# Batch 0 opened in a hand-written order of all engines, with a fence behind it

## The chip, the core and the metric

The kernel runs on one core of a Trainium2 chip. The core has five engines, each with its own instruction stream, executed in order: TensorE (PE in the profile, its weight loads PEld), VectorE (DVE), ScalarE (ACT), GpSimd (POOL) and SyncE (SP), which here issues transfers. Engines wait for each other through semaphores. The metric is the device time of one execution in microseconds (us); lower is better.

## The reference

Two layers over x of 4 batches x 512 tokens x 256 channels, all in float32. Cut to what matters:

```python
# layer 0: both branches start from xn = layernorm(x)
phi_q, phi_k = elu(q) + 1, elu(k) + 1              # q, k, v: 256 -> 256 each, with bias
context = phi_q * cumsum(phi_k * v, axis=1) * 0.25
attn = context @ Wo.T + bo
logits = (rms(xn) * norm_w) @ Wc.T / clip(temperature, 0.1)   # 512 "genes" per token
w = softmax(top_k(logits, 32))
e = sum_k w_k * genes[idx_k]                       # 32 numbers per token
ffn = tanh(e @ Wd.T) * xn' * (e @ Wu.T) * scale    # xn' = rms(xn) * norm_w
x = x + attn + ffn
# layer 1: both branches start from xn = layernorm(x)
q, k, v = split(rms(xn) @ w_qkv.T)
y = sigmoid(rms(q)) * cumsum(exp(rms(k)) * v) / (cumsum(exp(rms(k))) + 1e-6)
u, g = split(y @ w_swiglu.T)                       # 2 x 1024
mix = xn + (u * silu(g)) @ w_out.T
moe = two of 16 experts per token (176 wide) + a shared expert (352 wide)
x = x + mix + moe
```

The cumulative sums run along the 512 tokens of a batch, so the second half of a batch needs a carry from the first.

## The kernel before

Tokens lie in tiles of 128 (`P`), four (`NT`) to a batch; x stays in SBUF as `xs` for the whole kernel. The work is written as Python generators, and `together` takes steps from several of them in turn, so that their instructions stand interleaved in the program; a scheduler then orders each engine's instructions, and may move an instruction ahead of others that it does not depend on. So statistics of later batches can stand between steps of batch 0.

The generators:
- `layer0(b, i0, nt)` (L231) does layer 0 for `nt` tiles of batch b from tile i0: statistics and normalisation (`statistics` L201, `normalise` L218, on DVE), turned rows `xnT` through PE and ACT (`turn` L224), then for each tile `logits` (L293: four matmuls of which two reach one bank of PSUM at a time), `top` (L303: four rounds of max and match_replace on DVE, then the weights `e`), a share of the attention branch (`phi` L260, `attend_kv` L272, `attend_q` L285) and `express` (L320: `e` turned, multiplied with genes, then with Wd and Wu, tanh, and four GpSimd operations that add bias and branch to `xs`); at last `out` (L343), the out-projection added to `xs`.
- `mix(b, i0, nt)` (L368) is the mixing of layer 1: statistics, turned rows `xn1T`, q, k, v, sums, `yT`, and the router's weights. At its end it enters `(xnT, yT)` in `made` (L464).
- `dense(busy)` (L574) is the shared expert and the gated projection of layer 1, by halves of a batch (256 tokens). A half has 11 steps (`NC`): three chunks of the shared expert, which need only `xn1T` (weights `sgu`), and eight of the gated projection, which need `yT` (weights `wugt`). A step is `up` (four matmuls `gu`, L584, 256 columns each) and, two steps behind, `down` (two matmuls `acc`, L604). There are 8 halves, 88 steps in all; `d(n)` takes n of them.
- `route` and `scatter` (L467, L549) sort the tokens by expert; `scatter` writes 32 sets of rows to DRAM from GpSimd's queue. `experts` (L783) reads them in pairs of tiles (`xg`), turns them (L712), and multiplies with an expert's weights, `pu` (L749) and `py` (L770).
- The tail runs what is left of `dense`; in it GpSimd gathers the experts' rows 32 times (L885), asked for by step number, and DVE adds them to `xs` (L896), also by step number.

The calls that set the order are few:

```python
    together(a(0, 0, 2))
    together(m(0, 0, 2), a(0, 2, 2))
    ...
    together(m(0, 2, 2), a(1, 0, 4), d(NC))
    together(m(1, 0, 4), a(2, 0, 4), d(NC))
    together(m(2, 0, 4), a(3, 0, 4), d(NC))
    ...
    together((scatter(), 33), d(14))
    run_all(islice(dd, 2 * NC - 19))
    ...
    together((experts(), NP2 + 2))
```

Batch 0 comes in halves, so that the first mixing can start after two tiles. PSUM is in four banks `pm` (`bank`, L195), three `gu` and one `acc`. All loads are issued on SP's queue in the order of L103 to L151; small ones (`nwc`, `tmp1`, `bqkv`, `scl`) stand between large ones. DVE scales `wct` with the norm's weights (L157). The halvings of `wot1` and `sdn` (L648 to L650, on ACT) stand behind batch 0.

Of the kernel before, what the change touches and what calls it, by code (L numbers as in the profile page):

```python
# [2 lines left out]

# [51 lines left out]
def tile_two_layers(  # L55
# [53 lines left out]
    G.memset(ones, 1.0)  # L109

    load_x(0)
# [4 lines left out]
    nc.sync.dma_start(nwc, norm_w.rearrange("(h p) -> p h", p=P))  # L116
    tmp1 = wp.tile([P, 1], F32, name="tmp1")
    nc.sync.dma_start(tmp1, temperature.partition_broadcast(P))
    nc.sync.dma_start(wqkv, wqkv0.rearrange("(h p) e -> p h e", p=P))
    bqkv = wp.tile([P, 6], F32, name="bqkv")  # L120
    nc.sync.dma_start(bqkv, bqkv0)
# [7 lines left out]
    nc.sync.dma_start(scl, scale.partition_broadcast(P))  # L129
# [23 lines left out]
    V.tensor_scalar(nbqk, bqkv[:, 0:4], -1.0, None, ALU.mult)  # L153
    bqkv1 = wp.tile([P, 4], F32, name="bqkv1")
    V.tensor_scalar(bqkv1, bqkv[:, 0:4], 1.0, None, ALU.add)
    for h in range(NH):
        V.tensor_scalar(wct[:, h], wct[:, h], nwc[:, h : h + 1], None, ALU.mult)  # L157
    rtemp = wp.tile([P, 1], F32, name="rtemp")
    V.tensor_scalar(rtemp, tmp1, 0.1, None, ALU.max)
    V.reciprocal(rtemp, rtemp)  # L160
# [40 lines left out]
    def statistics(pool, b, i0, nt):  # L201

        mv = pool.tile([P, NT, 2], F32, name="mv")
        rs = pool.tile([P, 2, NT], F32, name="rs")
        ve = pool.tile([P, NT], F32, name="ve")
        for i in range(nt):
            bs = pool.tile([P, 6], F32, name="bs")
            V.bn_stats(bs, xs[:, b, i0 + i])
            V.bn_aggr(mv[:, i], bs)
        V.tensor_scalar(rs[:, 0, 0:nt], mv[:, 0:nt, 1], LN_EPS, None, ALU.add)  # L210
# [3 lines left out]
        S.activation(rs[:, :, 0:nt], rs[:, :, 0:nt], AF.Sqrt)  # L214
        V.reciprocal(rs[:, :, 0:nt], rs[:, :, 0:nt])
# [15 lines left out]
    def layer0(b, i0, nt):  # L231

        W = nt * P
        mv, rs = statistics(io, b, i0, nt)
        xn = io.tile([P, NT, D], F32, name="xn")
        normalise(xn, b, i0, nt, mv, rs)

        sl = io.tile([P, 2, NT], F32, name="sl")
        V.tensor_scalar(sl[:, 0, 0:nt], rs[:, 1, 0:nt], rtemp, None, ALU.mult)
        V.tensor_scalar(sl[:, 1, 0:nt], rs[:, 1, 0:nt], scl, None, ALU.mult)  # L240
        yield
        xnT = io.tile([P, NH, L], F32, name="xnT")
        for h in range(NH):
            S.copy(xnT[:, h, 0:W], turn(xn, nt, h * P))  # L244
        yield


        def project(c):
            pm = bank()[:, 0:W]
            for h in range(NH):  # L250
                T.matmul(  # L251
                    pm,
                    wqkv[:, h, c * P : (c + 1) * P],
                    xnT[:, h, 0:W],
                    start=(h == 0),
                    stop=(h == NH - 1),
                )
            return pm

        def phi(c):  # L260

            pm = project(c)
            e = io.tile([P, L], F32, name="phi", bufs=3)[:, 0:W]
            S.activation(e, pm, AF.Relu, bias=nbqk[:, c : c + 1], scale=-1.0)
            S.activation(e, e, AF.Exp, scale=-1.0)
            V.scalar_tensor_tensor(e, pm, bqkv1[:, c : c + 1], e, ALU.add, ALU.max)
            return e

        ctxT = one.tile([P, NH, L], F32, name="ctxT")
        cums = {}  # L270

        def attend_kv(h):  # L272
            fk = phi(2 + h)
            pv = project(4 + h)
# [9 lines left out]

        def attend_q(h):  # L285
            fq = phi(h)
            V.scalar_tensor_tensor(ctxT[:, h, 0:W], fq, QSCALE, cums[h], ALU.mult, ALU.mult)


        rden = io.tile([P, NT], F32, name="rden")  # L290
        exT = one.tile([P, L], F32, name="exT")

        def logits(i):  # L293
            pl = bank()
            for h in range(NH):
                T.matmul(  # L296
                    pl, xnT[:, h, i * P : (i + 1) * P], wct[:, h], start=(h == 0), stop=(h == NH - 1)
# [5 lines left out]
        def top(i, lg):  # L303
            tp = io.tile([P, NACT], F32, name="top")
            rep = io.tile([P, NG], F32, name="rep")
            for r in range(NACT // 8):
# [3 lines left out]
                if r == 0:  # L310
                    nm = io.tile([P, 1], F32, name="nm")
                    V.tensor_scalar(nm, tp[:, 0:1], sl[:, 0, i : i + 1], -1.0, ALU.mult, ALU.mult)
                    e = io.tile([P, NG], F32, name="e")
                    S.activation(e, lg, AF.Exp, bias=nm, scale=sl[:, 0, i : i + 1])
            den = io.tile([P, 1], F32, name="den")
            V.scalar_tensor_tensor(e, rep, TAKEN, e, ALU.is_equal, ALU.mult, accum_out=den)
            V.reciprocal(rden[:, i : i + 1], den)
            return e

        def express(i, e):  # L320
# [4 lines left out]
            S.copy(wT.rearrange("p c t -> p (c t)"), pw)  # L325
            px = bank()
            for c in range(NGC):
                T.matmul(px[c * GD : (c + 1) * GD, 0:P], gn[:, c], wT[:, c], start=True, stop=True)
            S.copy(exT[:, i * P : (i + 1) * P], px[:, 0:P])
            du = bank()  # L330
            T.matmul(du, exT[:, i * P : (i + 1) * P], wdut, start=True, stop=True)
            dn = io.tile([P, D], F32, name="dn")
            S.activation(dn, du[:, 0:D], AF.Tanh, scale=rden[:, i : i + 1])
            cf = io.tile([P, 1], F32, name="cf")
            V.tensor_tensor(cf, rden[:, i : i + 1], sl[:, 1, i : i + 1], ALU.mult)
            V.scalar_tensor_tensor(dn, du[:, D : 2 * D], cf, dn, ALU.mult, ALU.mult)
            xw = io.tile([P, D], F32, name="xw")
            G.tensor_tensor(xw, xn[:, i], nwb, ALU.mult)
            G.tensor_tensor(dn, dn, xw, ALU.mult)
            G.tensor_tensor(xs[:, b, i0 + i], xs[:, b, i0 + i], bob, ALU.add)  # L340
            G.tensor_tensor(xs[:, b, i0 + i], xs[:, b, i0 + i], dn, ALU.add)

        def out(i):  # L343
            ao = bank()[:, 0:D]
            for h in range(NH):
                T.matmul(  # L346
                    ao, ctxT[:, h, i * P : (i + 1) * P], wot[:, h], start=(h == 0), stop=(h == NH - 1)
                )
            V.tensor_tensor(xs[:, b, i0 + i], ao, xs[:, b, i0 + i], ALU.add)


        parts = [lambda h=h, f=f: f(h) for h in range(NH) for f in (attend_kv, attend_q)]
# [610 lines left out]
```

## Time and profile before

| what | value |
|---|---|
| median of 3 runs | 581.01 us (578.38 to 581.03) |
| the profiled execution | 576.85 us, its span 575.1 us |
| instructions in the profile | 7191 |
| weight loads on PE | 383.5 us (67%) |
| moved by transfers | 46.76 MB, mean 81 GB/s |

The page's first part gives each engine's busy time; its second cuts the span into 40 equal slices, each digit being the busy share of a slice in tenths, with the clock that PE was granted below. In the timeline a line has a start and a duration in us, then engine, line of the kernel and operation, the tile written and the tiles read, the shape and the count; in brackets stands how long the engine was idle before it and what ended the wait. A matmul in float32 leaves two records, a turn of 128x128 one. A line can belong to a helper: L228 is the turn wherever `turn` is called.

### The profile page before, as it was taken

To read this page: it belongs to the slowest core of one execution; us is meant where nothing else is said; L and a number is where in the kernel's file an instruction comes from. 1 tells how busy PE (TensorE), PEld (TensorE's weight loads), DVE (VectorE), ACT (ScalarE), POOL (GpSimd) and SP (SyncE) were. 2 spreads that over 40 slices of the span, in tenths; PEclk is the share of its full clock that TensorE was granted. 3 is DMA by queue.
4 is the path that set the end of the run, shared out by engine and by line. 5 is a ranking of instruction groups with operands and counts; after the bars stand their busy time and mean duration, and the time that the engine had idled before them with its cause. 6 is when DMAs were issued, how large, how long until landed. Compare 5 with 4: busy or idle time off the path is not lost.

```text
span 575.1 us, 7191 instructions
## 1 busy us (share of the span) xinstructions
PE 527.4 (92%) x2324; PEld 383.5 (67%) x2324; DVE 370.3 (64%) x985; ACT 228.4 (40%) x517; POOL 173.6 (30%) x214
## 2 busy tenths in 40 slices
PE   3557989989999999999999989997999999999996
PEld 1344656558656676566677768886677777788885
DVE  4979999998796797967981499232222222236653
ACT  1452746562655825458344611111433333321110
POOL 1235132354222423223352322774000000016660
PEclk9788899999999999999999999999899999999999
DMA  5995000000000000000045630233333332114441
GB/s 165 376 375 206 1 1 0 2 0 1 0 2 0 0 1 2 0 1 1 1 144 158 202 100 11 103 109 126 94 110 101 102 109 92 55 66 129 123 143 40
DMA packets 37736, 46.76 MB, mean 81 GB/s; under 512 B 3936, under 2 KB 34240, under 8 KB 37440
## 3 DMA queue, kind: packets, MB, share of 16 engines
q1 hardware_dynamic: 34624, 37.87, 20.2%
q0 software_dynamic: 3072, 8.39, 4.8%
q8 instruction: 20, 0.33, 0.2%
q14 instruction: 20, 0.16, 0.1%
HBM read 27.64 MB, written 18.61 MB: 80 GB/s over the span
## 4 chain that ended last, share of the span: by engine, by line
PE 54%; DVE 22%; POOL 8%; ACT 7%; issue 4%; DMA 4%; SPq 0%; POOLq 0%; ACTq 0%; DVEq 0%
PE gu L584 12%; PE pu L749 9%; PE acc L604 7%; PE py L770 6%; PE pm L391 5%; DVE rep L309 4%; DVE top L308 4%; POOL xrows L552 3%; PE pt L712 3%; POOL ys L885 3%; PE pm L251 3%; PE pm L296 2%; PE pm L228 2%; PE pm L346 2%; DVE sums L437 2%
## 5 line engine op out<-in xcount | busy, mean ns | idle before, releaser
L584 PE MATMUL gu<-yT,wugt 128*128 128x256 f32 x512 | 126.0, 381 | 0.0
L584 PEld LDWEIGHTS gu<-yT,wugt 128*128 128x128 f32 x512 | 94.9, 190 | 18.9 <-issue 7.2
L588 ACT ACTIVATE th<-gu 128x256 f32<-128x256 f32 (+1 forms) x88 | 33.5, 382 | 122.7 <-PE gu L584 116.1
L885 POOL DMA_INDIRECT ys<-yrows,slot x32 | 30.7, 961 | 133.4 <-PE gu L584 117.9
L604 PE MATMUL acc<-wot,hid 128*128 128x256 f32 x256 | 66.2, 381 | 0.4
L595 POOL TENSOR_TENSOR hid<-hid,th 128x256 f32<-128x256 f32 (+1 forms) x44 | 34.1, 779 | 101.2 <-ACT hid L594 97.9
L590 DVE SCALAR_TENSOR_TENSOR th<-th,gu 128x256 f32<-128x256 f32 (+1 forms) x88 | 36.1, 412 | 41.6 <-ACT th L588 41.5
L749 PE MATMUL pu<-wex,xgT 128*128 x168 | 58.3, 470 | 0.8 <-DMA xg<-xrows 0.8
L604 PEld LDWEIGHTS acc<-wot,hid 128*128 128x128 f32 x256 | 48.1, 190 | 9.3 <-POOL hid L595 2.0
L251 PE MATMUL pm<-xnT,wqkv 128*128 128x512 f32 (+1 forms) x120 | 46.7, 530 | 3.9 <-ACT qk L398 1.7
L584 PE MATMUL gu<-xn1T,sgu 128*128 128x256 f32 (+1 forms) x192 | 47.3, 382 | 1.4 <-ACT hid L594 1.3
L758 DVE TENSOR_TENSOR hb<-pu,hb 128x176 f32<-128x176 f32 x42 | 14.3, 341 | 51.9 <-ACT hb L757 51.9
L391 PE MATMUL pm<-w,xn1T 128*128 128x512 f32 (+1 forms) x128 | 45.9, 502 | 0.1
L584 PEld LDWEIGHTS gu<-xn1T,sgu 128*128 128x128 f32 (+1 forms) x192 | 33.8, 181 | 9.5 <-ACT hid L594 2.6
L770 PE MATMUL py<-wex,hgT 128*128 x168 | 39.8, 379 | 0.0
L391 PEld LDWEIGHTS pm<-w,xn1T 128*128 128x128 f32 x128 | 24.7, 194 | 21.7 <-issue 17.5
L251 PEld LDWEIGHTS pm<-xnT,wqkv 128*128 128x128 f32 x120 | 23.8, 201 | 21.9 <-issue 13.2
L770 PEld LDWEIGHTS py<-wex,hgT 128*128 128x128 f32 x168 | 31.8, 190 | 7.9 <-issue 0.4
L552 POOL DMA_INDIRECT xrows<-xn,slot x32 | 30.9, 966 | 19.7 <-DVE th L590 10.3
L749 PEld LDWEIGHTS pu<-wex,xgT 128*128 128x128 f32 x168 | 29.4, 195 | 10.5 <-ACT xgT L726 1.2
L762 DVE COPY hgT<-pt 128x512 f32<-128x512 f32 x21 | 14.5, 691 | 30.0 <-PE pt L712 30.0
L296 PE MATMUL pm<-wct,xnT 128*128 128x512 f32 x64 | 33.4, 659 | 0.3 <-ACT xnT L244 0.2
(163 smaller groups left out, 872.2 us busy)
## 6 DMA issues: line engine op xcount, KB each, us to landing
xrows<-zero SPq DMA_DIRECT2D x1, 6016.0 KB, 23.3
wex<-in_w_gate_up_dram SPq DMA_DIRECT2D x8, 704.0 KB, 4.7
xg<-xrows SPq DMA_DIRECT2D x21, 256.0 KB, 2.7
yrows<-yg SPq DMA_DIRECT2D x21, 256.0 KB, 2.1
xs<-in_x_dram SPq DMA_DIRECT2D x4, 512.0 KB, 8.0
wugt<-in_wug_dram SPq DMA_DIRECT2D x1, 2048.0 KB, 11.9
wex<-in_w_down_dram SPq DMA_DIRECT2D x4, 512.0 KB, 4.8
out_dram<-xs SPq DMA_DIRECT2D x7, 256.0 KB, 2.8
```

What stands on the lines that cost most here:

```text
L251: T.matmul(pm, wqkv[:, h, c * P : (c + 1) * P], xnT[:, h, 0:W], start=(h == 0), stop=(h == NH - 1),)
L296: T.matmul(pl, xnT[:, h, i * P : (i + 1) * P], wct[:, h], start=(h == 0), stop=(h == NH - 1))
L391: T.matmul(o[:, 0:n], xnT[:, h, i * P : (i + 1) * P], w1[:, h, at : at + n], start=(h == 0), stop=(h == NH - 1),)
L552: sc = G.indirect_dma_start(out=xrows, out_offset=bass.IndirectOffsetOnAxis(ap=slot[:, k, i : i + 1], axis=0), in_=xn1[:, i // NT, i % NT] ...
L584: T.matmul(gu[0:m, k], w[:, h, at : at + m], ins[which][:, h], start=(h == 0), stop=(h == NH - 1))
L588: S.activation(th[0:m], gu[0:m, 0], AF.Tanh, scale=0.5)
L590: V.scalar_tensor_tensor(th[0:m], th[0:m], 1.0, gu[0:m, 0], ALU.add, ALU.mult)
L595: G.tensor_tensor(hid[0:m], hid[0:m], th[0:m], ALU.mult)
L604: mm = T.matmul(acc[:, t], hid[0:m, t * P : (t + 1) * P], dw[0:m, dc], start=(n == 0 and t == 0), stop=(n == NC - 1), skip_group_check=True,)
L749: T.matmul(pg[:, 0 : 2 * NI], xT[:, i, h], wex[:, bass.ds(at[i] + h * 2 * NI, 2 * NI)], start=(h == 0), stop=(h == NH - 1),)
L770: mm = T.matmul(py[:, i * D : (i + 1) * D], hT[:, i, h], wex[:, bass.ds(at[i] + EW - (2 - h) * D, D)], start=(h == 0), stop=(h == 1),)
L885: G.indirect_dma_start(out=ys[:, asked], out_offset=None, in_=yrows, in_offset=bass.IndirectOffsetOnAxis(ap=slot[:, k, n : n + 1], axis=0) ...
```

## The change

Batch 0 is no longer given as two `layer0` generators. `parts0` holds the pieces of layer 0 for a range of tiles as separate functions, and `opening` calls them in an order written out by hand, for both halves of batch 0 up to the turned rows of the first mixing (two tiles). Within `tc.manual_schedule` PE, DVE, ACT and GpSimd keep that order; `tc.no_sync_barrier()` is a fence for the scheduler, which moves nothing across it. What is left of the first mixing and of batch 0's second half then runs through `together` as before, with three dense steps; the other batches are `layer0(b)` over four tiles.

Along with it: x of batch 0 is loaded in two pieces, and four small loads go from SP's queue to ACT's; `ones` is set by DVE instead of GpSimd, `wct` is scaled by GpSimd instead of DVE; matmuls of the identity into an unused bank (`keep_up`) stand in four places; the expressed rows of two tiles are made together (`express`); the two parts of `made` are entered as each becomes ready; two more dense steps run between scatter and experts (`2 * NC - 17`), and the adds of gathered rows in the tail are asked for earlier by step number (15 for 17).

```diff
-    G.memset(ones, 1.0)
-
-    load_x(0)
+    V.memset(ones, 1.0)
+
+    nc.sync.dma_start(xs[:, 0, 0:2], x[0, 0:HB].rearrange("(t p) d -> p t d", p=P))
...
     nc.sync.dma_start(wct, wc.rearrange("(h p) g -> p h g", p=P))
...
-    nc.sync.dma_start(nwc, norm_w.rearrange("(h p) -> p h", p=P))
+    nc.scalar.dma_start(nwc, norm_w.rearrange("(h p) -> p h", p=P))
+    nc.sync.dma_start(xs[:, 0, 2:4], x[0, HB:].rearrange("(t p) d -> p t d", p=P))
...
-        V.tensor_scalar(wct[:, h], wct[:, h], nwc[:, h : h + 1], None, ALU.mult)
+        G.tensor_scalar(wct[:, h], wct[:, h], nwc[:, h : h + 1], None, ALU.mult)
...
+        def express(i, wTs):
+            px = bank()
+            for c in range(2):
+                for g in range(NGC):
+                    j = g % 2 * 2 + c
+                    T.matmul(
+                        px[g * GD : (g + 1) * GD, 0:P], gn[:, j], wTs[g // 2][:, j], start=(c == 0), stop=(c == 1)
+                    )
+            exT = io.tile([P, P], F32, name="exT")
+            S.copy(exT, px[:, 0:P])
+            dus = [bank(), bank()]
+            for t, du in enumerate(dus):
+                half = slice(t * P // 2, (t + 1) * P // 2)
+                T.matmul(du, exT[half], wdut[half], start=True, stop=True)
+            for t, du in enumerate(dus):
+                expressed(i + t, du)
...
+    def opening():
+        k = batch0(0)
+        p, q = parts0(0, 0, 2, k), parts0(0, 2, 2, k)
+        idle = ps_a.tile([P, 2, D], F32, name="acc")
+
+        def keep_up(n):
+            for _ in range(n):
+                T.matmul(idle[:, 0, 0:P], ident, ident, start=True, stop=True)
+
+        keep_up(14)
+        mv = moments(io, 0, 0, 2)
+        rs = spread(io, mv, 2)
+        mv2 = moments(io, 0, 2, 2)
+        V.reciprocal(rs[:, :, 0:2], rs[:, :, 0:2])
+        normalise(k.xn[:, 0:2], 0, 0, 2, mv, rs)
+        p.turn_in()
+        rs2 = spread(io, mv2, 2)
...
+        p.scales(rs)
+        V.reciprocal(rs2[:, :, 0:2], rs2[:, :, 0:2])
+        normalise(k.xn[:, 2:4], 0, 2, 2, mv2, rs2)
...
+        q.scales(rs2)
+        lg = {0: p.logits(0), 1: p.logits(1)}
+        held = {}
+        for two in ((2, 4), (0, 3), (5, 1)):
+            pm = ps_d.tile([P, 2, HB], F32, name="gu")
+            for j, c in enumerate(two):
+                held[c] = p.project(c, pm[:, j])
+        low = {2: p.decay(2, held[2])}
+        e0 = p.top(0, lg[0])
+        for c in (0, 3):
+            low[c] = p.decay(c, held[c])
+        q.turn_in()
+        low[1] = p.decay(1, held[1])
+        lg[2] = q.logits(2)
+        w0 = p.turn_genes(e0)
+        e1 = p.top(1, lg[1])
+        lg[3] = q.logits(3)
+        keep_up(8)
+        w1t = p.turn_genes(e1)
+        p.sum_kv(0, p.phi(2, held[2], low[2]), held[4])
+        p.context(0, p.phi(0, held[0], low[0]))
+        kh = p.phi(3, held[3], low[3])
+        p.express(0, [w0, w1t])
+        keep_up(8)
+        p.sum_kv(1, kh, held[5])
+        p.context(1, p.phi(1, held[1], low[1]))
+        for c in range(0, DFF // P, 2):
+            S.mul(wot1[:, c : c + 2], wot1[:, c : c + 2], 0.5)
...
+        p.out(0)
+        p.out(1)
+        keep_up(12)
+        m0 = mix(0, 0, 2)
+        next(m0)
+        next(m0)
+        return m0, q.rest(lg)
...
-    together(a(0, 0, 2))
-    together(m(0, 0, 2), a(0, 2, 2))
...
-    together(m(0, 2, 2), a(1, 0, 4), d(NC))
...
+    kinds = mybir.EngineType
+    with tc.manual_schedule(engines={kinds.PE, kinds.DVE, kinds.Activation, kinds.Pool}):
+        m0, second = opening()
+    tc.no_sync_barrier()
+    run_all(islice(m0, 2))
+    together((m0, 4), (second, 8), d(3))
+    together(m(0, 2, 2), a(1), d(NC - 3))
+    together(m(1, 0, 4), a(2), d(NC))
+    together(m(2, 0, 4), a(3), d(NC))
...
-    run_all(islice(dd, 2 * NC - 19))
+    run_all(islice(dd, 2 * NC - 17))
...
-        while added < 2 * NTT and 17 * added <= 32 * (step - 3):
+        while added < 2 * NTT and 15 * added <= 32 * (step - 3):
```

`p` stands for tiles 0 and 1, `q` for tiles 2 and 3. `moments` and `spread` are the two halves of `statistics`, up to the square root on ACT; `decay` is the part of `phi` on ACT, `phi` what DVE does behind it; `turn_genes` is the turn of `e` with its copy; `rest` is the loop over tiles of `layer0`, with logits that are there already taken over.

## The prediction

> **What bounds the kernel now.** The page first. TensorE (PE) is busy for 92% of the span, and the two rows of slices say where it is not:
>
> ```profile
> PE 527.4 (92%) x2324; PEld 383.5 (67%) x2324; DVE 370.3 (64%) x985; ACT 228.4 (40%) x517; POOL 173.6 (30%) x214
> PE   3557989989999999999999989997999999999996
> DVE  4979999998796797967981499232222222236653
> PEclk9788899999999999999999999999899999999999
> ```
>
> The gaps of PE lie in the first six slices (14.4 us each) and in slice 28; there DVE is full, and the clock dips. Busy is not work, though: PE's records are long when its clock is low. So I made a ledger from the groups by line with their shapes kept apart: records in a stretch times what one takes when PE is warm (from the chain: eight 128x256 in 1.73 us, so 0.215; 0.43 for 512 columns, 0.11 for 128, 0.30 for 352). Time less that work is time lost: 9.7 us by 10 us, 24.0 by 40, 30.6 by 55, **36.2 by 85**; then nothing (33.5 to 36.5) as far as 280; 4.6 in 320 to 360; **7.2 in 398 to 410**; 5.4 in the last 15 us. Of 575.1 us some 520 are work. The change touches the two bold places.
>
> The timeline of PE, then that of DVE (start, duration):
>
> ```profile
> 9.32 1.14 PE L228 MATMUL pm<-ident,xn 128*128 128x128 f32 x4 [9.32 <-DVE xn L220]
> 10.49 5.72 PE L296 MATMUL pm<-wct,xnT 128*128 128x512 f32 x8
> ...
> 23.90 1.09 PE L323 MATMUL pm<-ident,e 128*128 128x128 f32 x4 [5.10 <-DVE carry L282]
> ...
> 44.25 1.22 PE L228 MATMUL pm<-ident,xn 128*128 128x128 f32 x4 [5.81 <-DVE xn L220]
> ```
>
> ```profile
> 14.92 0.69 DVE L308 MAX8 top<-lg 128x8 f32<-128x512 f32 x1 [2.88 <-ACT lg L300]
> ...
> 43.78 3.80 DVE L220 TENSOR_SCALAR xn<-xs,mv,rs 128x256 f32<-128x256 f32 x6
> ...
> 54.16 0.68 DVE L308 MAX8 top<-lg 128x8 f32<-128x512 f32 x1
> ```
>
> DVE is the opening's chain: top-32 of two tiles from 14.9, first mixing normalised at 44.4 (the first two of those six), top-32 of tiles 2 and 3 only at 54.2. From 39.6 to 54 DVE worked largely for batches 1 to 3: twelve bn_stats (0.33 each), eight normalisations and what goes with them, some 14 us with two scalings at 72.8, while PE idled.
>
> The seam to the experts:
>
> ```profile
> 396.26 0.96 POOL L552 DMA_INDIRECT xrows<-xn,slot  x1 [0.30 <-issue]
> ```
>
> ```profile
> 396.82 1.03 PE L604 MATMUL acc<-wot,hid 128*128 128x256 f32 x4
> 401.66 1.09 PE L712 MATMUL pt<-ident,xg 128*128 128x128 f32 x4 [3.81 <-DMA xg<-xrows]
> 403.50 2.71 PE L749 MATMUL pu<-wex,xgT 128*128 x4 [0.75 <-DMA xg<-xrows]
> ```
>
> Scatters run on POOL every 1.26 us, the last at 396.3; PE is out of dense work at 397.9, waits 3.8 us, and goes on at half speed (2.71 for what later takes 1.19).
>
> **The opening by the new order.** In-order engines, durations from those rows.
> - First rows: 256 KB instead of 512 come first. Loads of 256 KB (xg) land in 2.7 us, so 0.8+2.7 = 3.5, against 4.3. Moments and spread of two tiles 1.4, square root 0.3: 5.2. But the second moments stand in DVE's queue ahead of the first reciprocal, and their rows arrive behind wct: the same 1 MB had landed at 5.8 (wct: 1.3+4.5). So 5.8+0.8+0.15, reciprocal by 6.75, two normalisations by 8.0 at 0.62 each (the x6 row, beside POOL; 0.35 alone). Turn and copy 0.8: logits from 8.4 instead of 10.5.
> - wct's scaling goes from DVE (0.48 each) to POOL, whose form the trace does not show. nwc, moved to ACT's queue ahead of the table load, lands about 0.8+4.6 = 5.4. Nearest row: POOL's two-input 128x512 at 1.37, two by 8.2. The Trainium skill ("GPSIMD Engine Reference", Engine selection) speaks against it: elementwise belongs on VectorE, about twice as fast for two inputs; one-input is "roughly line-rate", which gives about 0.5 each. Either is in time for 8.4, so 0; late by more, it is on the chain one for one. Its "SBUF — State Buffer" (Who interferes with whom) is harsher: a 2-port DVE op is shut out for the whole POOL instruction, so the two normalisations could wait until 8.2, +1.2. The row's 0.62 is taken. Four issues of 0.47 and the table load of 1.28 leave ACT free at 4.0, before the root at 4.9. SP loses those four, so what it issues behind comes 0.5 to 2 earlier. The other three small loads, wqkv and ones on DVE land before their first reader: 0.
> - Fourteen dummy matmuls warm PE: two logits matmuls 1.7 (cold 2.9), lg copy 0.6. **Top-32 of tile 0 starts at 11.1, not 14.9.**
> - Written out, the two top-32s do not interleave. A dependent round took 1.52 (maxima at 25.96 and 27.48) against 1.27 when two alternate; with scale and sum 6.9 each: 18.0 and 24.9. The six projections (5.1 of PE), second turns and logits lie beside this.
> - Then the turn of e1 0.55, copy 0.6, px 0.4, exT 0.3, two du 1.8 (warm), tanh, dn: DVE at 28.8 and 29.7; phi, kv, scan, context of the halves end at 32.0, beside it.
> - POOL is late next: xw and the bias, done early before, now stand in order: from 28.9 seven ops of 0.73 end at **34.0** (before: 1.55 behind dn). Out-projection (32.1 to 33.9) is covered.
> - Residual add 0.5, statistics 1.5, square root 0.4, normalisation by 37.4; turned rows 38.4. The six halvings, now in ACT's order between tanh and the root, wait for wot1 (15.3+14.0 = 29.3, as tanh ends) and sdn (30.2), and need 3.2 plus 1.3 of table load: done by 34, needed at 36. The fence shows no instruction or wait of its own in the program's order.
>
> So first-mixing normalisation stands at 37.4 against 44.4, and top-32 of tiles 2 and 3 follows at once: **37.4 against 54.2, 16.8 us earlier**. From there to the end of the first mixing (85.0) DVE does the same, less 1.3 (a scaling of batch 2), plus 1.8 (moments of batch 1): 68.7, so 16.3 gained with the same PE work done. The 42 dummies (9 us warm) lie in waits.
>
> The clock: the skill ("TensorE: Matmul & The Clock Gate", Part 1) holds the warm-up below 1% of a typical span, here 5.8 us, so warming could bring no more; the records show 34.0 busy for 26.1 of work by 60 us, 7.9 of stretch alone. I take the records. If dummies do not warm it, about 5.5 of cold turns, logits, du, out return on the new chain: gain 10.8.
>
> **The debt.** Of the 14 us hoisted, 1.8 is counted. Batch 1 still owes about 4 in a stretch (85 to 120) with DVE 34 of 35 us busy and PE full; batches 2 and 3 about 7 where DVE is 80 to 90% busy. PE has eight dense steps (2.59 each) as cover. Between 0 and 11 I take 3.5, since PE has lost nothing there: **opening 12.8**.
>
> **Seam and tail.** 2NC-17 instead of 2NC-19 moves two steps, 5.2 us, ahead of the experts. Scatters still start with the same step, xg had landed 3.8 after PE stopped, so the wait goes and PE stays warm; the copy to xgT (0.75) and 0.2 stay: **6.2 of 7.2**. The tail has 20 steps. Gathers are asked for at the same steps, so the last still issues with step 18:
>
> ```profile
> 560.44 0.94 POOL L885 DMA_INDIRECT ys<-yrows,slot  x1 [0.40 <-DVE th L590]
> ```
>
> It lands near 563.0, and its add (15*added) stands in DVE's queue ahead of the last hidden product, which PE wants at 562.8: add 0.5, product 0.4, so **-0.7** (0 to -3).
>
> Halves expressed in pairs: eight exT copies (0.27) less on ACT, same PE columns; the first tile waits for the second. 0 behind dense steps, up to 3 at one stage's end without. `made` set early: three sgu steps were ahead before too, 0.
>
> Sum: 12.8 + 6.2 - 0.7 = 18.3. Profiled execution: 576.85 (span 575.1), so 558.5. The median of the runs is 581.01, 0.7% above: **562.5**.
>
> **Rivals.**
> 1. The debt is paid in full: DVE's idle up to 85 us was 14.1, the new order idles about 12 by its fence. For: DVE is as full as PE to 120. Against: slack later. 16.3-11 = 5.3; with 5.5 for the rest 10.8: 570. Chance 0.19.
> 2. Seam gives nothing, because scatters slip with the steps or the tail waits on gathers (1.26 us each leave six us in twenty steps): 12.8 alone, 568. For: the chain there is all POOL. Against: pacing showed only 0.3. Chance 0.10.
> 3. Debt hidden whole: 16.3+5.5, 559. Chance 0.15.
> 4. Slower: without the hoist, each later batch's statistics fall on its own chain (normalise, turn, logits, top-32), ahead of PE's cover. It decides from a payment of 22 us, and the hoisted rows sum to 14, so one and a half times over: at 25, 584. Chance 0.03.
> 5. The change does not do what it says: the order shortens the opening, but PE loses as much behind the fence, and the seam stays: 580. Chance 0.02.
>
> The forecast has 0.51. Its own range is 557 to 567. Landing times, POOL's two ops (+1.2) and cold PE (5.5) widen it; 556 to 571 leaves out the last two rivals and the edges. A measurement tells 0.5% (2.9 us): faster 0.94, same 0.02, slower 0.04.
>
> **What would show it.** First top-32 near 11, POOL's last add near 34, first-mixing rows turned near 38, next top-32 straight behind. L317 at 0.43 each, not 0.72. Lost work by the end of the first mixing near 20, then 3 to 4 more before 140. No wait for xg at the seam, first pu near 1.2. The last gather behind the last but one step, one short wait of PE at the end. Wrong if top-32 starts after 13, or if PE idles behind the fence for over 6 us.

## The result, and the profile after

| | changed kernel | kernel before |
|---|---|---|
| median of 7 runs | 574.62 us (572.46 to 576.04) | 580.86 us (578.38 to 581.52) |
| ratio, 95% interval | 0.9909 (0.9889 to 0.9929) | |
| profiled execution | 574.23 us, span 572.5 | 576.85 us, span 575.1 |

By the ratio of the runs the change brings about 5.3 us (the medians lie 6.2 apart); 18.3 were forecast, as 562.5 us with a range of 556 to 571. One run of the experiment `again` below, 915.54 us at a granted clock of 0.557, was slow and stands in none of the figures. The page of the changed kernel (busy times, then the rows of slices, 14.3 us each):

```profile
PE 531.6 (93%) x2408; PEld 390.4 (68%) x2408; DVE 370.1 (65%) x984; ACT 233.8 (41%) x515; POOL 172.8 (30%) x215
PE   6969789979899999999999989978999999999995
DVE  5979989999897897968942687313322222225554
PEclk8999989999999999999999999997999999999999
```

PE's gaps of the first six slices are smaller, but there is one again at the scatters (the 8, 9, 9, 7, 8 right of the middle of PE's row).

The opening, in the timelines of PE, DVE and POOL (start, duration, engine, line, operation):

```profile
1.64 4.73 PE L439 MATMUL acc<-ident 128*128 128x128 f32 x28 [1.64 <-POOL ident masks.py:199]
9.33 0.87 PE L235 MATMUL pm<-ident,xn 128*128 128x128 f32 x4 [2.95 <-DVE xn L227]
10.49 5.37 PE L317 MATMUL pm<-wct,xnT 128*128 128x512 f32 x8 [0.29 <-issue]
```

```profile
7.56 0.43 DVE L204 BATCH_NORM_STATS2 bs<-xs 128x6 f32<-128x256 f32 x1 [1.41 <-DMA xs<-in_x_dram]
...
8.83 0.77 DVE L227 TENSOR_SCALAR xn<-xs,mv,rs 128x256 f32<-128x256 f32 x2
9.52 0.57 DVE L212 TENSOR_SCALAR rs<-mv 128x2 f32<-128x2 f32 x1
...
14.09 0.69 DVE L329 MAX8 top<-lg 128x8 f32<-128x512 f32 x1 [1.50 <-ACT lg L321]
...
41.30 0.73 DVE L227 TENSOR_SCALAR xn<-xs,mv,rs 128x256 f32<-128x256 f32 x2
41.95 1.28 DVE L329 MAX8 top<-lg 128x8 f32<-128x512 f32 x2
```

```profile
6.89 3.17 POOL L158 TENSOR_SCALAR wct<-wct,nwc 128x512 f32<-128x512 f32 x2 [5.30 <-DMA wct<-in_wc_dram]
...
37.75 0.72 POOL L378 TENSOR_TENSOR xs<-xs,dn 128x256 f32<-128x256 f32 x1
```

The first top-32 starts at 14.09, hardly earlier than before (14.92) and 3 us behind the forecast, past the bound of 13 that the prediction had set itself. Two things stand behind it. The second moments waited for their rows until 7.56, so the reciprocal and the rows behind them came late (9.6). And PE, after its dummies (the matmuls of `keep_up`) and 2.95 us of idling, ran the logits slowly (5.37 for eight records, 0.67 each, 0.43 when warm; the granted clock was 0.64 from 10.5 to 13.5 us). POOL's scaling of `wct` ended at 10.06, late too, but ahead of the copy of the first turned rows on ACT (10.39), so it did not hold the logits up. The last residual term left POOL at 38.5, not 34.0, and the first mixing's rows stood at 42.0, not 37.4. Top-32 of tiles 2 and 3 follows at once: 12.2 us earlier than before, where 16.8 were forecast. In the four later profiles of this opening, `again`, `again_2`, `seam_back` and `seam_back_2`, it is 11.1 to 12.0.

At the seam the wait for the first expert rows is gone, and a new one stands ahead of it. ACT, PE and POOL during the scatters of the changed kernel, then PE at the first expert rows:

```profile
379.52 0.38 ACT L722 ACTIVATE th<-gu 128x256 f32<-128x256 f32 x1 [4.63 <-PE acc L738]
387.28 0.94 ACT L722 ACTIVATE th<-gu 128x256 f32<-128x256 f32 x3 [7.37 <-remote]
```

```profile
376.16 1.89 PE L714 MATMUL gu<-yT,wugt 128*128 128x256 f32 x8
...
388.63 2.08 PE L738 MATMUL acc<-wot,hid 128*128 128x256 f32 x4 [4.90 <-DVE hid L726]
390.50 3.43 PE L714 MATMUL gu<-yT,wugt 128*128 128x256 f32 x8
...
404.99 0.60 PE L844 MATMUL pt<-ident,xg 128*128 128x128 f32 x4
406.34 1.45 PE L881 MATMUL pu<-wex,xgT 128*128 x4 [0.75 <-ACT xgT L858]
```

```profile
383.86 0.96 POOL L682 DMA_INDIRECT xrows<-xn,slot  x1 [0.30 <-issue]
387.58 0.96 POOL L682 DMA_INDIRECT xrows<-xn,slot  x1 [2.76 <-remote]
```

ACT owes PE a tanh every 2.59 us. The first of the three at 387.28 takes the columns that PE had finished at 378.1 (`gu` at 376.16; each step has one tanh, and they come in the same order); yet ACT and POOL stood still and went on within 0.3 us of each other. Then PE waits 4.9 us and runs at half rate for some 5 (2.08 us for four records of `acc` that take 1.03 elsewhere). Below this is called **the stop**. The profile of before, on which the prediction was built, has none of it: there tanhs come every 2.59 us through all the scatters.

### The profile page after: what moved, and what is told of

It is laid out like the page before. It is cut to its first block, busy times and chain, and to the rows that moved or that the text cites. A ratio compares the mean times of both kernels' runs of the same rounds, so it can differ in the third digit from the quotient of the medians.

```text
span 572.5 us, 7344 instructions
## 1 busy us (share of the span) xinstructions
PE 531.6 (93%) x2408; PEld 390.4 (68%) x2408; DVE 370.1 (65%) x984; ACT 233.8 (41%) x515; POOL 172.8 (30%) x215
## 4 chain that ended last, share of the span: by engine, by line
PE 51%; DVE 29%; POOL 7%; issue 5%; ACT 3%; DMA 2%; another core or an unknown queue 1%; SPq 0%; POOLq 0%; ACTq 0%; DVEq 0%
PE gu L714 12%; PE pu L881 9%; PE acc L738 7%; PE py L902 6%; POOL ys L1017 5%; DVE rep L330 4%; DVE top L329 4%; PE pm L520 4%; PE pt L844 3%; DVE sums L568 3%; PE pm L317 3%; PE pm L268 3%; DVE sums L557 2%; DVE xn L227 2%; PE pm L235 2%
## 5 line engine op out<-in xcount | busy, mean ns | idle before, releaser
L714 PE MATMUL gu<-yT,wugt 128*128 128x256 f32 x512 | 128.2, 387 | 0.0
L714 PEld LDWEIGHTS gu<-yT,wugt 128*128 128x128 f32 x512 | 96.5, 194 | 18.9 <-issue 6.6
L738 PE MATMUL acc<-wot,hid 128*128 128x256 f32 x256 | 67.9, 387 | 6.8 <-DVE hid L726 5.7
L729 POOL TENSOR_TENSOR hid<-hid,th 128x256 f32<-128x256 f32 (+1 forms) x44 | 32.7, 745 | 127.1 <-ACT hid L728 123.8
L881 PE MATMUL pu<-wex,xgT 128*128 x168 | 56.9, 461 | 0.8 <-ACT xgT L858 0.8
L890 DVE TENSOR_TENSOR hb<-pu,hb 128x176 f32<-128x176 f32 x42 | 14.3, 341 | 45.1 <-ACT hb L889 45.1
L268 PE MATMUL pm<-xnT,wqkv 128*128 128x512 f32 (+1 forms) x96 | 38.5, 540 | 1.8 <-DVE sums L557 1.8
L881 PEld LDWEIGHTS pu<-wex,xgT 128*128 128x128 f32 x168 | 28.6, 190 | 10.1 <-ACT xgT L858 1.0
L728 ACT COPY hid<-gu 128x256 f32<-128x256 f32 (+1 forms) x44 | 16.3, 374 | 41.7 <-DVE th L724 36.3
L329 DVE MAX8 top<-rep 128x8 f32<-128x512 f32 x48 | 32.8, 687 | 0.4
```

The source lines that it names most:

```text
L268: T.matmul(pm, wqkv[:, h, c * P : (c + 1) * P], k.xnT[:, h, tok], start=(h == 0), stop=(h == NH - 1),)
L329: V.max(tp[:, 8 * r : 8 * r + 8], src)
L714: T.matmul(gu[0:m, k], w[:, h, at : at + m], ins[which][:, h, t0 : t0 + HB], start=(h == 0), stop=(h == NH - 1),)
L729: G.tensor_tensor(hid[0:m], hid[0:m], th[0:m], ALU.mult)
L738: mm = T.matmul(acc[:, t], hid[0:m, t * P : (t + 1) * P], dw[0:m, dc], start=(n == 0 and t == 0), stop=(n == NC - 1), skip_group_check=True,)
L881: T.matmul(pg[:, 0 : 2 * NI], xT[:, i, h], wex[:, bass.ds(at[i] + h * 2 * NI, 2 * NI)], start=(h == 0), stop=(h == NH - 1),)
```

## The experiments

Eighteen kernels, two of them the changed kernel again, ran in five groups; those of a group ran on one chip beside runs of the kernel before. That kernel's median was 580.1 us in the first group and 576.3, 576.7, 576.5 and 575.8 in the others. So a kernel is compared within its group, by its ratio to before, or with kernels of the last four groups, whose medians of before lie within 0.9 us; the 95% intervals reach about 1 us either way, so between groups a difference below some 2 us is not clear of the noise. The planner, in what follows, is the scheduler that orders each engine's instructions.

### The seam, and the stop

One profile had shown the stop. Whether it belongs to the changed kernel, to its seam or to that execution decides what the seam is worth. The changed kernel again; its seam as before; the seam alone on the kernel before:

```diff
-    run_all(islice(dd, 2 * NC - 17))
+    run_all(islice(dd, 2 * NC - 19))
-        while added < 2 * NTT and 15 * added <= 32 * (step - 3):
+        while added < 2 * NTT and 17 * added <= 32 * (step - 3):
```

(`seam_back`; `seam_alone` is the same edit the other way round, on the kernel before.)

> The changed kernel once more, nothing edited. Two theories of the seam. Stall theory: the stop of ACT during the scatters (no tanh for 7.4 us at 380 to 387, PE waiting 4.9 us at 388.6 and then at half rate) comes with the changed kernel each time, and has eaten the seam's gain: it is there again in this profile, and the time is 574 to 576. Chance theory: it belonged to that one execution: tanhs come every 2.6 us through the scatters, PE waits less than 1 us there, and the profiled execution lies 3 to 5 us below the earlier 574.2, or the median of the timed runs does.

> The changed kernel with the seam as before (19 steps kept out, adds paced by 17). Stall theory (seam worth nothing or a little less): 573 to 576, as the changed kernel, all of the gain of 5.3 being the opening's. Chance theory (seam worth its 6): 579 to 581, the opening worth nothing. Either way PE waits some 3.8 us for the first expert rows again.

> The kernel before with the seam's two numbers alone (17 and 15). Stall theory: 580 to 583, no gain. Chance theory: 574.5 to 576, a gain of 5 to 6 and no wait for the first expert rows.

Measured: again 575.02 us, ratio 0.9917 (0.9889 to 0.9944); seam_back 576.31, 0.9939 (0.9918 to 0.9960); seam_alone 580.52, 0.9993 (0.9974 to 1.0012). The stop was in all three profiles, and the seam was worth 1.3 us in one pair, which is within the noise, and nothing in the other. The stop is no property of the new seam: seam_back has it, and so has fence_alone (below), whose program at the scatters is that of before. PE in fence_alone, with before's seam:

```profile
388.30 1.89 PE L584 MATMUL gu<-yT,wugt 128*128 128x256 f32 x8
395.60 2.08 PE L604 MATMUL acc<-wot,hid 128*128 128x256 f32 x4 [5.41 <-DVE hid L592]
397.47 2.97 PE L584 MATMUL gu<-yT,wugt 128*128 128x256 f32 x8
```

It stands behind the 26th scatter again, POOL's gap 2.7 us. While PE stands, scatters go on, so their end is no longer waited for: the wait of 3.8 us that the seam's two steps were to cover had been taken already. Contrary to the expectation, seam_back has no such wait, nor has fence_alone (at the first expert rows PE waits 0.75 us in each).

The four profiles of the second group were without the stop, so the pair was run once more:

> The changed kernel once more. The stop in the scatters was in the five profiles of two chips, and in none of the four of a third, where the kernel before took 576 instead of 580. Chip theory: the stop belongs to the chip; where this profile has it, the ratio to before is 0.991 again, and where it has not, 0.980 to 0.983 (some 565), since the seam then gives its 5 to 6. Rival (the seam gives nothing anywhere): 0.991 without the stop too.

> The changed kernel with the seam as before, beside again_2 on its chip. Chip theory: without the stop, PE waits 3.8 us for the first expert rows and the kernel is 4 to 6 slower than again_2; with the stop, within 1.5 of it. Rival: within 1.5 either way.

Measured: again_2 566.63 us, 0.9817 (0.9799 to 0.9835); seam_back_2 571.60, 0.9915 (0.9900 to 0.9931). Neither profile has the stop. PE at the first expert rows in seam_back_2, then in again_2:

```profile
395.86 1.09 PE L844 MATMUL pt<-ident,xg 128*128 128x128 f32 x4 [3.82 <-DMA xg<-xrows]
397.70 2.71 PE L881 MATMUL pu<-wex,xgT 128*128 x4 [0.75 <-DMA xg<-xrows]
```

```profile
398.04 0.60 PE L844 MATMUL pt<-ident,xg 128*128 128x128 f32 x4
399.39 1.45 PE L881 MATMUL pu<-wex,xgT 128*128 x4 [0.75 <-ACT xgT L858]
```

So **without the stop the seam is worth 5.0 us, and with it 1.3 at most**. The chip theory falls in its name: the first and the third group ran on the same chip. The stop goes with the group of runs, not with the kernel: all 14 profiles of the later groups are free of it, all four of the first have it. That before's runs of the first group had it too is read from their times (580.1 against some 576, and 580.5 in fence_alone, which has it), not seen.

### What the opening is worth, by the microsecond

Four edits touch the opening alone. Behind the opening their profiles show, engine by engine, the same instructions in the same order as the changed kernel's, so they move one thing: when the opening ends.

late4, eight more memsets on DVE (and 16 more dummies beside them):

```diff
+        for _ in range(8):
+            V.memset(ones, 1.0)
         e1 = p.top(1, lg[1])
```

> The changed kernel with eight memsets of a 128x512 tile (0.48 each, 3.9 us of DVE) put ahead of the second top-32 of the opening, and 16 more dummy matmuls beside them. DVE theory (DVE's queue bounds all of the first 120 us, so each microsecond on it in the opening counts one for one): 3 to 4.5 us slower than the changed kernel, 578.5 to 580. Cover theory (by 120 us PE has dense work to fill in, and the opening's end is worth little): less than 1.5 slower.

first_chain, the order that the prediction had thought of, with `wct` back on DVE and 18 dummies first instead of 14:

```diff
-        mv2 = moments(io, 0, 2, 2)
         V.reciprocal(rs[:, :, 0:2], rs[:, :, 0:2])
         normalise(k.xn[:, 0:2], 0, 0, 2, mv, rs)
         p.turn_in()
+        for h in range(NH):
+            V.tensor_scalar(wct[:, h], wct[:, h], nwc[:, h : h + 1], None, ALU.mult)
+        mv2 = moments(io, 0, 2, 2)
```

> The changed kernel with the opening's first chain as the prediction had thought of it: the moments of tiles 2 and 3 behind the normalised rows of tiles 0 and 1, wct scaled on DVE behind those (0.48 each) instead of on POOL (1.58 each), 18 dummy matmuls instead of 14. First top-32 at 11 instead of 14.1. DVE theory: 2.5 to 3.5 us faster than the changed kernel. Cover theory: within 1.

cold leaves out the dummies (`keep_up` does nothing):

> The changed kernel without its 42 dummy matmuls. Clock theory (they keep PE at full rate where the chain runs over it: turns, logits of tiles 2 and 3, expression, out-projection, mixing's rows): 3 to 5.5 us slower than again_2. Rival (the first logits are at half rate with them too, and the rest waits on DVE): less than 1.5 slower.

best1 goes on from first_chain, with 15 dummies first: `tops` runs two top-32s in turn, `ready` puts POOL's two independent operations ahead. Cut:

```diff
-        p.express(0, [w0, w1t])
-        keep_up(8)
         p.sum_kv(1, kh, held[5])
+        p.express(0, [w0, w1t], xws)
+        keep_up(8)
...
-        e0 = p.top(0, lg[0])
+        e0, e1 = p.tops((0, 1), lg)
...
+        xws = [p.ready(0), p.ready(1)]
```

> The kernel of first_chain with 15 dummies first instead of 18, the two top-32s of the opening taken in turn, POOL's factor rows and bias adds moved ahead of the gated rows, and the second sum ahead of them on DVE. The first mixing's normalised rows come at 34 to 35.5 instead of 39.2 (41.3 in the changed kernel). DVE theory (one for one): 5 to 7 us faster than again_2 on the same chip, 558 to 561 where there is no stop. Cover theory: no faster than first_chain, 563 to 565.

In the table, the rows are the start of the first mixing's two normalisations in DVE's timeline, the shifts are against again_2, and the medians of late4 and first_chain come from another group without the stop:

| kernel | rows at | shift | median, us | difference | ratio to before, 95% |
|---|---|---|---|---|---|
| again_2 | 42.38 | | 566.63 | | 0.9817 (0.9799 to 0.9835) |
| late4 | 47.41 | +5.0 | 571.72 | +5.1 | 0.9926 (0.9907 to 0.9944) |
| cold | 43.47 | +1.1 | 568.76 | +2.1 | 0.9859 (0.9839 to 0.9878) |
| first_chain | 39.19 | -3.2 | 563.91 | -2.7 | 0.9787 (0.9766 to 0.9808) |
| best1 | 35.95 | -6.4 | 559.92 | -6.7 | 0.9719 (0.9700 to 0.9738) |

The time follows the end of the opening about one for one, both ways. The agreement is good to about 1 us: in five profiles of the changed kernel's opening the rows start between 41.3 and 42.4. In late4 each memset takes 0.48 and waits 0.17 for the last one, which writes the same tile, hence 5.0 and not 3.9 for eight. The dummies are worth 2.1 us here, where the first logits ran slowly with them too (4.89 us for eight in again_2, 5.74 in cold), and **best1 beats both kernels**: 16.8 us under the kernel before. DVE and PE in best1, with the wait for the second piece of x and the cold logits gone:

```profile
6.65 0.74 DVE L225 TENSOR_SCALAR xn<-xs,mv,rs 128x256 f32<-128x256 f32 x2
7.38 0.88 DVE L477 TENSOR_SCALAR wct<-wct,nwc 128x512 f32<-128x512 f32 x2
...
35.95 0.73 DVE L225 TENSOR_SCALAR xn<-xs,mv,rs 128x256 f32<-128x256 f32 x2
```

```profile
8.23 3.70 PE L315 MATMUL pm<-wct,xnT 128*128 128x512 f32 x8 [0.24 <-ACT xnT L259]
```

### Where the lead of 12 us goes

seam_back_2 has the opening without the seam: 571.60 against 576.70, **5.1 us** for a lead of 11.3 us at the next top-32 (12.2 in the first profile). Three events along the way, each the end of a mixing's second `yT` in DVE's timeline:

| end of | before | again_2 | lead |
|---|---|---|---|
| first mixing (tiles 0, 1) | 83.7 | 70.8 | 12.9 |
| second mixing (tiles 2, 3) | 138.7 | 139.2 | -0.5 |
| third mixing (batch 1) | 217.3 | 213.1 | 4.2 |

All of it is lost between the first and the second mixing, where batch 1 runs its first layer; then PE, which meanwhile did some more dense work, is 4 us ahead. The changed kernel's first profile, again, seam_back and seam_back_2 say the same: 13.0 to 14.0 us at the first of these ends, -0.4 to 1.6 at the second, 4.3 to 6.2 at the third. The busy times of that stretch (stretch, length, then PE, PEld, DVE, ACT and POOL), in before and in again_2:

```profile
83.70:138.70 55.00, 53.08 (x226) 33.18 (x225) 54.02 (x153) 31.10 (x67) 23.04 (x30) 1.00 0.00 1
```

```profile
70.80:139.20 68.40, 62.78 (x269) 39.54 (x270) 65.51 (x179) 40.04 (x78) 27.30 (x37) 0.95 0.00 1
```

DVE is busy for 54.0 of 55.0 us and for 65.5 of 68.4: 11.5 us more work in the stretch. From 0 to the second mixing's end it sums to 123.6 and 123.8, the same. The hoisted work has come back on DVE in full, and 2 us of idling with it. Whether it could be kept from costing, nine kernels asked.

fence_alone, the kernel before with the fence:

```diff
-    together(m(0, 0, 2), a(0, 2, 2))
+    (m0, _), (second, _) = m(0, 0, 2), a(0, 2, 2)
+    for stream in (m0, second):
+        next(stream)
+        next(stream)
+    tc.no_sync_barrier()
+    together((m0, 6), (second, 8))
```

> The kernel before with nothing but the fence, set behind the first two steps of the first mixing and of tiles 2 and 3, so that the statistics of batches 1 to 3 no longer stand in DVE's queue ahead of top-32 of tiles 2 and 3, which starts some 8 to 10 us earlier. Debt theory (that work only filled idle DVE time, and DVE is full up to 110 or 140 us without it too, so it is owed again at once): within 2.5 us of the kernel before. Rival (the hoist itself held PE back, and PE has cover for it later): 569 to 574, 7 to 12 us faster.

Measured: 580.45 us, 1.0006 (0.9993 to 1.0019). It didn't put the question: the planner set the moments of batches 1 and 2 right behind the fence, and top-32 started at 52.9 instead of 54.2. It tells only that the fence alone, at that place, is worth nothing.

nostats_before and nostats_after leave out the moments and the spread of the later batches in the first layer (constants stand for them):

```diff
-        mv, rs = statistics(io, b, 0, NT)
+        mv, rs = mvc, io.tile([P, 2, NT], F32, name="rs")
+        S.activation(rs, rsc, AF.Sqrt)
```

> The kernel before without the moments and the spread of batches 1 to 3 in the first layer (constants stand for mean and variance; the square roots stay): twelve bn_stats and aggregates and what goes with them, some 8.5 us of DVE, leave the stretch of 39.6 to 54. Debt theory (there they filled time in which DVE had nothing else): at most 1.5 us faster than the kernel before. DVE theory (DVE bounds both kernels to 120 us, filled or not): 4 to 8 faster.

> The changed kernel without the same work (moments and spread of batches 1 to 3 left out). Debt theory (what filled idle time before is owed in full behind the fence): 5 to 8 us faster than the changed kernel, 567 to 570. DVE theory: 4 to 8 too. Cover theory (PE has dense work beside it): at most 1.5 faster.

Measured: nostats_before 574.66 us against 576.32, 0.9972 (0.9957 to 0.9987), 1.7 faster, about the bound of the debt theory (1.5); nostats_after 570.45, 0.9875 (0.9847 to 0.9902), which is 3.8 *slower* than again_2. All expectations for it missed, but not all of the 3.8 is sure: two of its six runs, at a mean clock of 0.987, took 567.0, the other four, at 0.977, some 570.6. The planner, given less work, had laid another order behind the opening; PE waits 3.5 us for sums there and 3.8 for turned rows of batch 1, and DVE is busy for only 56.8 of the 68.6 us between the mixings. A full DVE is thus not the whole of it.

no_fence takes away `tc.no_sync_barrier()` from the changed kernel:

> The changed kernel without its fence and with nothing else edited: the planner may again put later work into the opening's queues, and its order has the top-32 of tiles 2 and 3 between the opening's DVE steps, and moments of later batches among its last ones. Filling theory (what the fence costs is DVE time left idle in the opening, some 8 us, that is owed behind it): 3 to 6 us faster than the changed kernel (561 to 564; 570 to 573 with the stop). Standing-in-the-way theory (each step put in delays the first mixing one for one): 2 to 6 slower.

Measured: 575.07 us, 0.9974 (0.9963 to 0.9986), 8.4 slower than again_2, more than either theory allowed (the profiled execution, at 572.71, is the fastest of 22 and shows some 6 of the 8.4). Top-32 of tiles 2 and 3 and moments of later batches stood in the opening's queues again, and PE waited for the opening twice:

```profile
39.68 2.93 PE L383 MATMUL pm<-wot,ctxT 128*128 128x256 f32 x6 [5.16 <-DVE ctxT L302]
...
50.05 1.13 PE L235 MATMUL pm<-ident,xn 128*128 128x128 f32 x4 [4.65 <-DVE xn L227]
```

So in the changed kernel the fence is worth 8 us; on the kernel before, where it held nothing back, nothing.

act_norm, best2 and best3 move normalised rows of batches 1 to 3 to ACT: in the first layer of the changed kernel, of best1, and in both layers of best1.

```diff
+            V.scalar_tensor_tensor(off[:, 0:nt], mv[:, 0:nt, 0], -1.0, rs[:, 0, 0:nt], ALU.mult, ALU.mult)
+            for i in range(nt):
+                S.activation(to[:, i], xs[:, b, i0 + i], AF.Identity, bias=off[:, i : i + 1], scale=rs[:, 0, i : i + 1])
```

> The changed kernel with the normalised rows of batches 1 to 3 in the first layer written by ACT (scale and bias by row) instead of by DVE: twelve operations of 0.41 to 0.6 leave DVE behind the fence, three small ones come. Debt theory (DVE's work that was hoisted before is what PE waits for behind the fence): 2 to 5 us faster than the changed kernel, and no wait of PE for normalised rows near 80 (2.5 there now). Rival (the planner's order behind the fence, not DVE's load, sets those waits): within 1.5 either way, or slower by what the new order brings.

> The kernel of best1 with the same twelve normalised rows on ACT. Debt theory: 2 to 5 us faster than best1, 555 to 558. Rival: within 1.5 of best1.

> The kernel of best2 with the normalised rows of the second layer's mixings of batches 1 to 3 on ACT too. Debt theory (DVE full to 140): 1 to 3 us faster than best2. Rival: ACT's table loads and its own queue take it back, within 1 of best2 or slower.

Measured: act_norm 568.48 us, 0.9850 (0.9827 to 0.9873); best2 561.83, 0.9747 (0.9729 to 0.9766); best3 563.70, 0.9780 (0.9761 to 0.9799): 1.9, 1.9 and 3.8 slower than again_2 and best1. The first two are not clear of the noise; that the rows on ACT brought no gain is. DVE got its time back (61.4 busy between act_norm's mixings) and spent 6.4 of it waiting for batch 1's first logits. What PE waited for, in act_norm:

```profile
PE acc L744 <- POOL hid L735: 3.9, 1, 3.9
PE pm L241 <- ACT xn L230: 2.5, 1, 2.5
```

Near 80 us ACT has the square roots of two batches, the four rows (2.06) and tanhs of dense steps, with four table loads of 1.28 between 78 and 88; PE's columns wait for ACT and then POOL.

early1 and best1_early1 begin batch 1's moments, rows and turns one stage earlier:

```diff
-    together((m0, 4), (second, 8), d(3))
-    together(m(0, 2, 2), a(1), d(NC - 3))
+    a1 = layer0(1)
+    together((m0, 4), (second, 8), (islice(a1, 2), 2), d(3))
+    together(m(0, 2, 2), (a1, 16), d(NC - 3))
```

> The changed kernel with the first two steps of batch 1's first layer (moments, normalised rows, turns) begun one stage earlier, beside the top-32 of tiles 2 and 3 and behind the fence, instead of beside the second mixing. Batch-1 theory (the lead is lost at 75 to 95 because batch 1's chain of moments, rows, turns, logits starts only there, where before it stood ready since 53): no wait of PE for rows near 80, batch 1's first top-32 4 to 8 us earlier, 2 to 4 us faster than the changed kernel (562.5 to 564.5; 571 to 573 with the stop). Rival (whatever is put beside top-32 of tiles 2 and 3 holds up the first mixing and what follows it): within 1 or up to 4 slower.

> The kernel of best1 with the same edit. Batch-1 theory: 2 to 4 us faster than best1, 556 to 558. Rival: within 1 of best1's 560 or up to 4 slower.

Measured: early1 569.68 us, 0.9884 (0.9867 to 0.9902); best1_early1 564.08, 0.9798 (0.9777 to 0.9819): 3.1 and 4.2 slower. PE's wait for batch 1's rows went (0.2 left), and one of 3.2 for the weights `e` of batch 1 took its place; the first mixing ended at 73.9 instead of 70.8, the second at 138.8, where it had been in before and in again_2.

What follows: that the lead is lost in this stretch, and that the hoisted DVE work stands in it, is shown; that DVE's load alone sets its length is refuted, and so is the late start of batch 1 as the one cause. Less DVE work, ACT in DVE's place, and an earlier batch 1 each came with another order by the planner and other waits of the same size. Which chain sets the stretch in the order as it is stays open.

## Why the prediction was wrong

Two steps failed: the opening's term of 12.8 us, of which 5.1 came, and the step from one profiled execution to the runs, which took no stop into account. The seam's term held where there was no stop.

**The base.** The sum was made on an execution without the stop and then raised by 0.7% to the median of runs that, by their times, mostly had it. Without it the kernel before takes 576.5, as its profile said, and the changed kernel 566.6: a gain of 10.1. With it the changed kernel loses 8.0 more (574.62 against 566.63; 8.4 by `again`) and the one before some 4 (580.1 against 576.3), for in before the stop lies over a wait that was there anyway. The 12.1 us from 562.5 to 574.6 are thus 8.1 of gain that did not come (558.5 forecast for an execution like the profiled one, 566.6 measured), 8.0 of stop (566.6 to 574.6), less the 4.0 of the raise.

**The opening, 12.8, failed: 5.1.** It was the sum of a lead of 16.3 at the end of the first mixing and a debt of 3.5. In seam_back_2, which has the opening without the seam, the lead is 13.0 and 7.9 of it is lost again: 3.3 us are missing in the lead and 4.4 in the debt. By the terms of the lead:
- *First rows.* The piece of x came at 4.18 instead of 3.5, and the second one at 7.56 instead of 5.8; the prediction had seen the second moments stand in the queue and mis-sized their rows' landing by 1.8 us. With the slow logits below, this puts the first top-32 3.0 late; the terms given for it, 8.4, 1.7 and 0.6, add up to 10.7 and not to the 11.1 named.
- *`wct` on POOL at no cost.* "Either is in time" for 8.4 failed: the scaling ended at 10.06. `wct` itself came 1.5 us later than POOL's start had been put (6.89, not 5.4), and the operations took 1.58 each, not 1.37 or 0.5. The row of a two-input operation and the Trainium skill's "roughly line-rate" ("GPSIMD Engine Reference", Engine selection) were both too low, and its advice to keep it on VectorE was right. In the changed kernel the late rows hid this; with the rows at 8.4 it would, by these times, have been on the chain. The harsher rule ("SBUF — State Buffer", Who interferes with whom), priced at +1.2, shows in part: the two normalisations took 0.44 and 0.40 in the middle of POOL's second operation, but the small scaling behind them (the line at 9.52) took 0.57 instead of 0.17 and ended with POOL's. In ten of the eleven profiles with `wct` on POOL it took 0.56 to 0.60 and ended within 0.03 us of POOL's end; in the eleventh, late4, it was the first normalisation, with 0.79 instead of 0.41. So DVE lost some 0.4 us, mostly off the first chain.
- *The dummies.* They warm PE, but 14 ended at 6.4, and the logits behind them ran slowly. The skill ("TensorE: Matmul & The Clock Gate", Part 1) puts the return to half rate at an idle window of about 3.4 us; here less was enough, and the length of the gap alone does not decide: eight logits took 5.37 us after gaps of 2.95 and of 1.52 (again), but 3.67 after one of 2.71 (no_fence). best1's 15 end as the rows come, and its logits take 3.70 for eight. Their price, put at 5.5, is 2.1.
- *Top-32s* of 6.9 each: 7.3 and 6.9 (14.09, 21.4, 28.3). Right. *POOL's seven operations*: 5.5 instead of 5.1, and 4 late by what went before. Right in kind.
- So the next top-32 came 11.1 to 12.2 earlier instead of 16.8. Of the 4.6 to 5.7 missing there, 3.3 were still missing at the end of the first mixing.

*The debt of 3.5* ("since PE has lost nothing there") was 7.9. The work came back on DVE in full (rival 1, which put its cost at 11), but PE got some 3 us of dense work out of the time: 127 records of `gu` and `acc` by the end of the second mixing in again_2, 112 in before, at 0.215 us. Behind the fence PE waits for 10 us up to 123 in again_2, over the 6 set as a bound. The slip was to take PE's past as proof of cover: it had lost nothing from 85 to 120 with batch 1's rows ready since 53. That this readiness was the reason is argued, not shown: early1, which starts batch 1 sooner, did not bring the time back.

**The seam, 6.2, was right where the profile was right**: the wait goes, PE stays warm, the first `pu` is at 1.45 for four records (2.71 before), and seam and tail together bring 5.0 where 5.5 were forecast. That executions could lack the wait was not among the rivals. *The tail's -0.7*: PE waits 0.71 us for the last hidden product in again_2, as put; from the experts' last product to the end it takes 60.1 us, and 63.9 in seam_back_2, which is 3.8 saved for 5.2 us of steps moved, so 1.4 lost, in the range given.

**Rivals.** 1 comes nearest: its gain of 10.8 is about the 10.1 measured without the stop. That is luck in part, for the lead was shorter than it took (13.0, not 16.3) and so was the debt (7.9, not 11). 2 came true in the runs of the result for a reason it didn't name. 3 and 5 are out. 4, slower, is out for this kernel, but its mechanism, later batches' statistics on their own chain, is what the waits for batch 1's rows are (2.5 us in again_2).

## What to carry to other kernels

A profile is one execution: where its time lies well off the median of the runs, find out which part differs before a wait in it is priced, and run it a second time. When work is kept from filling idle time, follow it to where it goes and look at every engine of that stretch; slack that an engine shows there was made with the work already done. In a chain written by hand, set the instruction that waits for the later transfer behind those that don't need it: here that, with `wct`'s scaling moved off POOL, the two top-32s in turn and POOL's own part ahead, was worth 6.7 us, more than the whole opening had brought.

## What was not expected of the hardware

- The stop: ACT and POOL stand still during the scatters, ACT for 7.4 us in two profiles and 9.5 in three, POOL for 2.2 behind the 12th and 2.7 to 2.8 behind the 26th of 32 scatters. All five profiles that have it agree in this, and the 15 others, the same program among both, have none of it. The profile names "remote" as what ended the waits behind the 26th; the cause is open.
- POOL's one-input scaling of 128x512 took 1.58 us, longer than its two-input operation of that size (1.27), and 3.3 times DVE's 0.48. A small operation of DVE beside it ended with it, 0.4 us late, while others beside it did not wait.
- The same first instructions of PE, 14 dummies, turns and logits, took 5.37 us for the eight logits records after 1.52 us of idling in one execution, and 3.67 after 2.71 us in another.
- With the order behind it fixed, a kernel's time followed the end of its opening one for one over 11 us; changes of a few per cent of the work that let the planner order anew moved it by 2 to 8 us, mostly to the worse.
